# Non-local blocks: layers alternate between images, and the next block's keys and values are made inside the current one

## The chip, the cores and the metric

The kernel runs on one core of one Trainium2 chip. The metric is the device time of one execution in microseconds. Times of several runs are given as their median; one more execution was recorded by the hardware profiler, and all durations below come from that one.

## What is computed

Four images of 128 channels and 96x96 positions pass through two layers of the same form. Cut to one layer, with float32 throughout:

```python
g_x = maxpool2(conv1x1(x, g_w, g_b)).reshape(b, CI, -1).transpose(0, 2, 1)
theta_x = conv1x1(x, theta_w, theta_b).reshape(b, CI, -1).transpose(0, 2, 1)
phi_x = maxpool2(conv1x1(x, phi_w, phi_b)).reshape(b, CI, -1)
f = jnp.einsum('bqc,bck->bqk', theta_x, phi_x)
attn = jax.nn.softmax(f, axis=-1)
y = jnp.einsum('bqk,bkc->bqc', attn, g_x)
y = y.transpose(0, 2, 1).reshape(b, CI, H, W)
W_y = conv1x1(y, W_w, W_b)
inv = bn_gamma * jax.lax.rsqrt(bn_var + BN_EPS)
W_y = W_y * inv[None, :, None, None] + (bn_beta - bn_mean * inv)[None, :, None, None]
return W_y + x
```

CI is 64. An image has 9216 queries and, after the pooling, 2304 keys. Layer 1 reads what layer 0 wrote, so one image's two layers are strictly one after the other; different images do not depend on each other.

## The kernel before

One layer of one image is a *block*; there are eight, in the order image 0 layer 0, image 0 layer 1, image 1 layer 0 and so on (L322 to L326). An image is one SBUF tile x of 128 partitions x 9216, loaded in six pieces (L84); layer 0 writes its result back into it, layer 1 into a tile `out` that is stored (L286).

A block first makes its keys and values (`keys_and_values`, L146). In 24 chunks of 384 positions, `pooled` projects x to g and phi with one matmul of 128x128 weights (L157) into a PSUM buffer of the pool `ps_sc`, and VectorE takes the 2x2 maximum out of PSUM into `gphi` (L160). Three times, after 8 chunks each, `spread` brings phi onto both halves of the partitions on ScalarE (L174, L177, after a centre on VectorE, L170) and transposes g with six TensorE transposes (L180), which VectorE adds the bias to (L183).

Then the block goes over 9 *pairs* of 512 queries (NP, p). `theta` (L198) projects a pair's queries: two matmuls of 128x64 weights, one for each 512 queries, side by side in the array's columns. For each of 18 key tiles (k), `scores` (L219) issues four matmuls in 64x64 quarters of the array, ScalarE takes the exponential of the 128x1024 result (L228), VectorE adds it to a running sum (L232, L234), and `values` (L236) multiplies it by g, again in four 64x64 quarters, into the accumulator `av`. The loop in `block` (L297) goes in steps t of two key tiles: the scores of step t, then the values of step t-1. So TensorE alternates between 16 recorded passes of scores and 16 of values. (A float32 matmul is recorded as two passes.)

Behind a pair come its ending steps. ScalarE copies the accumulator out (`halves`, L249). `denominators` (L251), hung one step behind the pair's last values, sums the sums over partitions with a matrix of ones (`den`, two 128x64 matmuls, L254); VectorE takes four reciprocals from PSUM (L260), adds the halves (L262), multiplies (L263) and keeps a running largest and smallest reciprocal (L264, L265), from which a flag is made at the end that chooses a general routine if the sums went out of range. `project` (L267), three steps later, multiplies by W in two 64x128 matmuls (L275), and VectorE adds shift and x (L281). `theta` of the next pair is called in the middle of a pair. A scheduler of the language places the instructions of each engine by its own estimates; the order in the program is its input. The endings of a block's last pair fall into the next block's key making.

PSUM: `ps_sc` has two buffers of two banks, `ps_av` one of two, and `ps_misc` two of one bank, which `theta`, `den`, `W_ps` and `gT_ps` take in turn.

Of the kernel before, what the change touches and what calls it, by code (L numbers as in the profile page):

```python
# [16 lines left out]
P = 128  # L17
# [18 lines left out]
NB = NKT // KB  # L36
SHIFT = 35.0
# [4 lines left out]
def shifted_blocks(ctx: ExitStack, tc: tile.TileContext, x: bass.AP, layers, out: bass.AP, flag):  # L42
# [11 lines left out]

    nc = tc.nc
# [3 lines left out]
    xp = ctx.enter_context(tc.tile_pool(name="xp", bufs=2))  # L59
# [14 lines left out]
    rmax = const.tile([P, QT], F32, name="rmax")  # L74
    nc.gpsimd.memset(rmax, 1.0)
    rmin = const.tile([P, QT], F32, name="rmin")
    nc.gpsimd.memset(rmin, 1.0)
# [68 lines left out]
    def keys_and_values(xt, w, name):  # L146

        gphi = kvp.tile([P, NK], F32, tag="gphi", name=f"gphi_{name}", bufs=1)  # L150
        phi = kvp.tile([P, NK], F32, tag="phi", name=f"phi_{name}")
        gT = kvp.tile([P, NKT, CI], F32, tag="gT", name=f"gT_{name}")
        centre = kvp.tile([P, 1], F32, tag="centre", name=f"centre_{name}")

        def pooled(r):
            ps = ps_sc.tile([P, PT], F32, tag="sc", name=f"gphi_ps_{name}_{r}")
            nc.tensor.matmul(  # L157
                ps[:, :CC], lhsT=w["gphi"], rhs=xt[:, ts(r, CC)], start=True, stop=True
            )
            nc.vector.tensor_reduce(  # L160
                gphi[:, ts(r, CC // 4)].rearrange("p (h w) -> p h w", w=W // 2),
                ps[:, :CC].rearrange("p (h a w b) -> p h w a b", a=2, b=2, w=W // 2),
                AX.XY,
                ALU.max,
            )

        def spread(i):
# [10 lines left out]
            ps = ps_misc.tile([P, QT], F32, tag="misc", name=f"gT_ps_{name}_{i}")  # L178
            for j in range(GT):
# [4 lines left out]
                gT[:, ts(i, GT), :],  # L184
                ps[:, : GT * CI].rearrange("p (t c) -> p t c", c=CI),
                w["g_b"].rearrange("p (o c) -> p o c", o=1).to_broadcast((P, GT, CI)),
# [3 lines left out]
        per = GT * KT * 4 // CC  # L190
        for r in range(HW // CC):
            pooled(r)
            if r % per == 0 and r:
                spread(r // per - 1)
        spread(NKT // GT - 1)
        return phi, gT

    def theta(xt, w, p, name):  # L198
        ps = ps_misc.tile([P, QT], F32, tag="misc", name=f"theta_ps_{name}_{p}")
        for h in range(2):  # L200
            nc.tensor.matmul(  # L201
                ps[ts(h, CI), :], lhsT=w["theta"], rhs=xt[:, ts(2 * p + h, QT)],
# [439 lines left out]
```

## Time and profile before

| | |
|---|---|
| median of 3 runs | 2765.25 us (2764.35 to 2766.28) |
| the profiled execution, own time | 2764.58 us |
| its span in the profile | 2762.3 us |
| TensorE matmul (PE) busy | 2689.1 us, 97% |
| VectorE (DVE) busy | 2115.4 us, 77% |
| ScalarE (ACT) busy | 1536.5 us, 56% |
| DMA | 41.41 MB, mean 15 GB/s |

The span is the time from the profile's first instruction to its last; 2.3 us of the execution lie outside it. In the views, PE is TensorE's matmuls and PEld its weight loads, which have a row of their own; L12 is a line of the kernel, `av<-exp,gT` says which tile an instruction writes and which it reads. A row of the timeline has a start, the busy time of a group of equal instructions, the engine, line, operation, tiles, and the size of one; "x16" is how many, and in brackets stands how long the engine had been idle and who ended that. A matmul's recorded end is modelled and reaches into its successor, so the cost of a group of matmuls is read from its start to the start of the next. "64*64" is the part of the array that a matmul uses.

### The profile page before, as it was taken

The numbers are of one execution on the slowest core, as the hardware profiler recorded it, in microseconds if no ns is written. First come the engines' busy times: TensorE is split into PE (matmuls) and PEld (weight loads), VectorE is DVE, ScalarE is ACT, GpSimd is POOL, SyncE is SP. The second block draws the span as 40 slices with busy tenths as digits, with TensorE's granted clock in tenths as the row PEclk, the third lists the DMA queues.
The fourth block names the chain that finished last, engine by engine and source line by source line (L and its number), as shares of the span: only waits on it lengthen the run. The fifth ranks groups of instructions, "written<-read, shape, count | busy, mean of one in ns | idle before, by whom it ended". The sixth has DMA issues, their size and how long they took to land.

```text
span 2762.3 us, 50645 instructions
## 1 busy us (share of the span) xinstructions
PE 2689.1 (97%) x22136; PEld 911.1 (33%) x22136; DVE 2115.4 (77%) x2203; ACT 1536.5 (56%) x1492; POOL 1.6 (0%) x8
## 2 busy tenths in 40 slices
PE   7999999999999999999999999999999999999998
PEld 2333333333333333333333333333333333333332
DVE  4777767778677786777867778677786877867777
ACT  3555546555455564555546665455554666456664
POOL 0000000000000000000000000000000000000000
PEclk9999999999999999999999999999999999999999
DMA  4000000000100000000010000000000000000000
GB/s 142 1 1 1 1 1 16 16 17 17 77 1 1 1 1 1 16 17 16 16 77 1 1 1 1 1 17 16 16 17 9 1 1 1 1 1 17 16 16 25
DMA packets 11686, 41.41 MB, mean 15 GB/s; under 512 B 3392, under 2 KB 3776, under 8 KB 11456
## 3 DMA queue, kind: packets, MB, share of 16 engines
q1 hardware_dynamic: 8640, 37.75, 3.5%
q8 instruction: 175, 2.87, 0.4%
q10 hardware_dynamic: 2816, 0.34, 0.1%
q14 instruction: 55, 0.45, 0.1%
HBM read 19.21 MB, written 18.87 MB: 14 GB/s over the span
## 4 chain that ended last, share of the span: by engine, by line
PE 95%; DVE 2%; ACT 1%; DMA 1%; issue 0%; ACTq 0%
PE av L242 41%; PE sc L223 41%; PE gphi_ps L157 5%; PE W_ps L275 3%; PE theta_ps L201 3%; PE den L254 3%; DVE rc L260 1%; PE gT_ps L180 1%; DVE gphi L160 0%; ACT exp L228 0%; DMA W_nat<-in_L_conv_W_w_dram 0%; DVE centre L170 0%; ACT phi L174 0%; ACT phi L177 0%; DMA theta_b<-in_L_conv_theta_b_dram 0%; DMA theta_nat<-in_L_conv_theta_w_dram 0%
## 5 line engine op out<-in xcount | busy, mean ns | idle before, releaser
L228 ACT ACTIVATE exp<-sc,nshift 128x1024 f32<-128x1024 f32 x1296 | 1375.3, 1113 | 835.9 <-PE sc L223 835.7
L234 DVE TENSOR_TENSOR sum<-sum,exp 128x1024 f32<-128x1024 f32 x1152 | 1405.2, 1220 | 365.9 <-ACT exp L228 304.4
L223 PE MATMUL sc<-theta,phi 64*64 64x512 f32 x10368 | 1237.4, 592 | 13.0 <-ACT exp L228 8.4
L242 PE MATMUL av<-exp,gT 64*64 64x512 f32 x10368 | 1230.7, 590 | 0.0
L223 PEld LDWEIGHTS sc<-theta,phi 64*64 64x64 f32 x10368 | 381.6, 133 | 763.2 <-issue 735.7
L242 PEld LDWEIGHTS av<-exp,gT 64*64 64x64 f32 x10368 | 390.0, 133 | 729.2 <-issue 710.2
L260 DVE RECIPROCAL rc<-den 128x128 f32<-128x128 f32 x288 | 243.7, 908 | 12.6 <-PE den L254 12.6
L232 DVE TENSOR_TENSOR sum<-exp,exp 128x1024 f32<-128x1024 f32 x72 | 88.2, 1225 | 153.3 <-ACT exp L228 153.3
L157 PE MATMUL gphi_ps<-x,gphiT 128*128 128x384 f32 x384 | 172.0, 564 | 10.3 <-DVE gphi L160 5.2
L160 DVE TENSOR_REDUCE gphi<-gphi_ps 128x96 f32<-128x384 f32 x192 | 105.4, 556 | 62.3 <-PE gphi_ps L157 56.6
L206 ACT ACTIVATE theta<-theta_ps,theta_b 128x512 f32<-128x512 f32 x72 | 49.5, 688 | 148.5 <-PE theta_ps L201 148.5
L275 PE MATMUL W_ps<-y,WT 64*128 64x512 f32 x288 | 88.9, 696 | 31.5 <-DVE y L263 31.5
L174 ACT ACTIVATE phi<-gphi,centre 64x768 f32<-64x768 f32 x24 | 22.3, 930 | 153.8 <-DVE centre L171 119.4
L249 ACT COPY halves<-av 128x1024 f32<-128x1024 f32 x72 | 72.9, 1012 | 46.4 <-PE av L242 46.4
L157 PEld LDWEIGHTS gphi_ps<-x,gphiT 128*128 128x128 f32 x384 | 69.0, 208 | 78.5 <-DVE gphi L160 46.1
L201 PE MATMUL theta_ps<-x,thetaT 128*64 128x512 f32 x288 | 87.3, 618 | 0.0
L254 PE MATMUL den<-sum,ones 128*64 128x512 f32 x288 | 77.7, 618 | 0.0
L262 DVE TENSOR_TENSOR y<-halves 128x512 f32<-128x512 f32 x72 | 49.3, 685 | 15.5 <-ACT halves L249 15.5
L281 DVE SCALAR_TENSOR_TENSOR x<-W_ps,shift,x 128x512 f32<-128x512 f32 x72 | 53.3, 744 | 2.5 <-PE W_ps L275 2.5
L281 DVE SCALAR_TENSOR_TENSOR out<-W_ps,shift,x 128x512 f32<-128x512 f32 x72 | 53.3, 744 | 2.1 <-PE W_ps L275 2.1
L275 PEld LDWEIGHTS W_ps<-y,WT 64*128 64x128 f32 x288 | 23.3, 198 | 88.6 <-issue 51.2
L265 DVE TENSOR_TENSOR rmin<-rmin,rc 128x512 f32<-128x512 f32 x72 | 49.2, 684 | 0.0
(47 smaller groups left out, 230.1 us busy)
## 6 DMA issues: line engine op xcount, KB each, us to landing
x<-in_x_dram SPq DMA_DIRECT2D x24, 768.0 KB, 8.0
out_dram<-out SPq DMA_DIRECT2D x36, 512.0 KB, 2.6
theta_nat<-in_L_conv_theta_w_dram ACTq DMA_DIRECT2D x2, 32.0 KB, 5.5
theta_b<-in_L_conv_theta_b_dram ACTq DMA_DIRECT2D x4, 0.2 KB, 6.1
gphi_nat<-in_L_conv_g_w_dram ACTq DMA_DIRECT2D x2, 32.0 KB, 5.6
gphi_nat<-in_L_conv_phi_w_dram ACTq DMA_DIRECT2D x2, 32.0 KB, 5.2
g_b<-in_L_conv_g_b_dram ACTq DMA_DIRECT2D x2, 32.0 KB, 5.6
W_nat<-in_L_conv_W_w_dram ACTq DMA_DIRECT2D x2, 32.0 KB, 6.4
```

What stands on the lines that cost most here:

```text
L157: nc.tensor.matmul(ps[:, :CC], lhsT=w["gphi"], rhs=xt[:, ts(r, CC)], start=True, stop=True)
L160: nc.vector.tensor_reduce(gphi[:, ts(r, CC // 4)].rearrange("p (h w) -> p h w", w=W // 2), ps[:, :CC].rearrange("p (h a w b) -> p h w a b" ...
L201: nc.tensor.matmul(ps[ts(h, CI), :], lhsT=w["theta"], rhs=xt[:, ts(2 * p + h, QT)], start=True, stop=True,)
L223: nc.tensor.matmul(ps[ts(c, CI), ts(h, QT)], lhsT=self.phi[ts(h, CI), ts(2 * k + c, CI)], rhs=self.th[ts(h, CI), :], start=True, stop=True,)
L228: nc.scalar.activation(e, ps, AF.Exp, bias=nshift)
L232: nc.vector.tensor_add(self.sum, self.es[0], e)
L234: nc.vector.tensor_add(self.sum, self.sum, e)
L242: nc.tensor.matmul(self.av[ts(h, CI), ts(r, QT)], lhsT=self.gT[ts(r, CI), k, :], rhs=e[ts(r, CI), ts(h, QT)], start=(k == 0), stop=(k == N ...
L254: nc.tensor.matmul(ps[ts(h, CI), :], lhsT=ones, rhs=self.sum[:, ts(h, QT)], start=True, stop=True,)
L260: nc.vector.reciprocal(rc[:, ts(i, P)], ps[:, ts(i, P)])
L275: nc.tensor.matmul(ps, lhsT=self.w["W"][ts(h, CI), :], rhs=self.y[ts(h, CI), :], start=True, stop=True,)
L281: nc.vector.scalar_tensor_tensor(dst[:, ts(h, QT)], pss[h], self.w["shift"], self.xt[:, ts(2 * self.p + h, QT)], op0=ALU.add, op1=ALU.add,)
```

## The change

The diff does the following.

- The blocks come in the order of `ORDER`, so that a block of another image stands between the two layers of an image. Three x tiles are kept instead of two, and both layers write into x in place; the stores read x.
- The eight blocks become one loop over 72 pairs (of 9 steps each). Block n+1's keys and values are made while block n's pairs run: each pair has one *window*, behind the first values of that pair (`J_WINDOW`), in which its predecessor's `den`, three chunks of the next block's `pooled`, and the next pair's `theta` are issued together. A block's three `spread` steps are issued in the windows of its predecessor's pairs 3, 6 and 8; pair 8 has no chunks. The first block's keys are made ahead of the loop, and the last block has no next one to make.
- `pooled` uses two matmuls of 128x64 weights (the g and the phi half) in place of one of 128x128, and its PSUM comes from `ps_misc`, like all that a window writes.
- `den` is copied out of PSUM by ScalarE (`rc`); the reciprocals then read SBUF, and the extremes are two reductions into a column for each pair. All of it stands as one run on VectorE (`normalise`), behind the window's reductions.
- `project` uses four matmuls in 64x64 quarters and comes four steps after the window.
- `exp` has 9 buffers instead of 6; `halves` and `rc` have one instead of two.
- In the loop, TensorE, VectorE and ScalarE keep the order in which the program calls them (`manual_schedule`); the key making ahead of it is still placed by the scheduler. There, TensorE now has the weight transposes of both layers (L102, six of them) ahead of the first chunk; before, ten chunks stood ahead of the last of these (L97, `WT_ps` of layer 1).

The core of the diff:

```diff
+J_WINDOW, J_PROJECT = 0, 4
+CHUNKS = 3
+ORDER = ((0, 0), (1, 0), (0, 1), (2, 0), (1, 1), (3, 0), (2, 1), (3, 1))
...
-    xp = ctx.enter_context(tc.tile_pool(name="xp", bufs=2))
+    xp = ctx.enter_context(tc.tile_pool(name="xp", bufs=3))
...
-            ps = ps_sc.tile([P, PT], F32, tag="sc", name=f"gphi_ps_{name}_{r}")
-            nc.tensor.matmul(
-                ps[:, :CC], lhsT=w["gphi"], rhs=xt[:, ts(r, CC)], start=True, stop=True
-            )
+            ps = ps_misc.tile([P, QT], F32, tag="misc", name=f"gphi_ps_{self.name}_{r}")
+            for h in range(2):
+                nc.tensor.matmul(
+                    ps[ts(h, CI), :CC], lhsT=self.w["gphi"][:, ts(h, CI)],
+                    rhs=self.xt[:, ts(r, CC)], start=True, stop=True,
+                )
...
+        def key_steps(self):
+
+            steps = {}
+            for r in range(HW // CC):
+                steps.setdefault(r // CHUNKS, []).append(lambda r=r: self.pooled(r))
+            for i in range(NKT // GT):
+                last = ((i + 1) * GT * KT * 4 // CC - 1) // CHUNKS
+                steps.setdefault(last + 1, []).append(lambda i=i: self.spread(i))
+            return steps
...
-            rc = work.tile([P, QT], F32, tag="rc", name=f"rc_{self.name}")
+            self.rc = work.tile([P, QT], F32, tag="rc", name=f"rc_{self.name}", bufs=1)
+            nc.scalar.copy(self.rc, ps)
+
+        def normalise(self):
+            rc, n = self.rc, self.number
+            self.y = y = self.halves[:, :QT]
+            nc.vector.tensor_add(y, y, self.halves[:, QT:])
             for i in range(QT // P):
-                nc.vector.reciprocal(rc[:, ts(i, P)], ps[:, ts(i, P)])
...
-            nc.vector.tensor_tensor(rmax, rmax, rc, ALU.max)
-            nc.vector.tensor_tensor(rmin, rmin, rc, ALU.min)
+                nc.vector.reciprocal(rc[:, ts(i, P)], rc[:, ts(i, P)])
+            nc.vector.tensor_mul(y, y, rc)
+            nc.vector.tensor_reduce(rmax[:, n : n + 1], rc, AX.X, ALU.max)
+            nc.vector.tensor_reduce(rmin[:, n : n + 1], rc, AX.X, ALU.min)
...
-                ps = ps_misc.tile([P, QT], F32, tag="misc", name=f"W_ps_{self.name}_{h}")
-                nc.tensor.matmul(
-                    ps, lhsT=self.w["W"][ts(h, CI), :], rhs=self.y[ts(h, CI), :],
-                    start=True, stop=True,
-                )
-                pss.append(ps)
-            for h in range(2):
+                pss.append(ps_misc.tile([P, QT], F32, tag="misc", name=f"W_ps_{self.name}_{h}"))
+            for c in range(2):
+                for h in range(2):
+                    nc.tensor.matmul(
+                        pss[h][ts(c, CI), :], lhsT=self.blk.w["W"][ts(h, CI), ts(c, CI)],
+                        rhs=self.y[ts(h, CI), :], start=True, stop=True,
+                    )
...
+    with tc.manual_schedule(engines=engines):
+        for t in range(total + NB):
+            if t < total:
+                q, j = divmod(t, NB)
+                if q % NP == 0 and j == 0 and q // NP + 1 < len(blocks):
+                    begin(q // NP + 1)
+                    steps = blocks[q // NP + 1].key_steps()
                 for k in range(j * KB, (j + 1) * KB):
...
+                    pairs[q].scores(k)
+            if t == 0:
+                continue
+            q, j = divmod(t - 1, NB)
+            if j == J_PROJECT and q:
+                pairs[q - 1].project()
+            if t <= total:
                 for k in range(j * KB, (j + 1) * KB):
...
+                    pairs[q].values(k)
+            if j == J_WINDOW:
+                others = list(steps.pop(q % NP, [])) if q < len(pairs) else []
+                if q:
+                    pairs[q - 1].denominators()
+                for step in others[:1]:
+                    step()
+                if q + 1 < len(pairs):
+                    pairs[q + 1].theta()
+                for step in others[1:]:
+                    step()
+                if q:
+                    pairs[q - 1].normalise()
```

What that makes of the engines' orders, at three places. First TensorE inside the first block, where pair 2 has just begun. Before, the end of pair 1 (`den_0_0_1`: image 0, layer 0, pair 1; the last number is the buffer's) stands by itself between values (`av`) and scores (`sc`):

```order
L242 MATMUL av_0_0_2_814<-exp_0_0_2_0_777,gT_0_0_204 64x512 x4
L242 MATMUL av_0_0_2_814<-exp_0_0_2_1_784,gT_0_0_204 64x512 x4
L254 MATMUL den_0_0_1_823<-sum_0_0_1_543,ones_92 64x512 x2
L223 MATMUL sc_0_0_2_4_836<-theta_0_0_2_698,phi_0_0_203 64x512 x4
L223 MATMUL sc_0_0_2_5_844<-theta_0_0_2_698,phi_0_0_203 64x512 x4
```

Now, at the same place:

```order
L258 MATMUL av_0_0_2_868<-exp_0_0_2_0_831,gT_0_0_195 64x512 x4
L258 MATMUL av_0_0_2_868<-exp_0_0_2_1_838,gT_0_0_195 64x512 x4
L270 MATMUL den_ps_0_0_1_877<-sum_0_0_1_583,ones_92 64x512 x2
L168 MATMUL gphi_ps_1_0_6_882<-x_1_332,gphiT_0_117 64x384 x2
L227 MATMUL theta_ps_0_0_3_886<-x_0_96,thetaT_0_107 64x512 x2
L168 MATMUL gphi_ps_1_0_7_891<-x_1_332,gphiT_0_117 64x384 x2
L168 MATMUL gphi_ps_1_0_8_895<-x_1_332,gphiT_0_117 64x384 x2
L238 MATMUL sc_0_0_2_4_907<-theta_0_0_2_632,phi_0_0_194 64x512 x4
L238 MATMUL sc_0_0_2_5_915<-theta_0_0_2_632,phi_0_0_194 64x512 x4
```

Three chunks of image 1's keys (`gphi_ps_1_0_6` to `_8`) and the theta of pair 3, which stood nineteen rows behind `den`, have come into one run with `den`.

Second, TensorE where the first block ends. Before, from the last values of pair 8 on:

```order
L242 MATMUL av_0_0_8_2272<-exp_0_0_8_16_2449,gT_0_0_204 64x512 x4
L242 MATMUL av_0_0_8_2272<-exp_0_0_8_17_2457,gT_0_0_204 64x512 x4
L254 MATMUL den_0_0_8_2478<-sum_0_0_8_2244,ones_92 64x512 x2
L157 MATMUL gphi_ps_0_1_0_2501<-x_0_98,gphiT_1_164 128x384
L157 MATMUL gphi_ps_0_1_1_2504<-x_0_98,gphiT_1_164 128x384
L275 MATMUL W_ps_0_0_8_0_2491<-y_0_0_8_2486,WT_0_147 128x512
L275 MATMUL W_ps_0_0_8_1_2493<-y_0_0_8_2486,WT_0_147 128x512
L157 MATMUL gphi_ps_0_1_2_2507<-x_0_98,gphiT_1_164 128x384
L157 MATMUL gphi_ps_0_1_3_2510<-x_0_98,gphiT_1_164 128x384
L180 MATMUL gT_ps_0_1_0_2532<-ident_83,gphi_0_1_2497 128x64
L157 MATMUL gphi_ps_0_1_4_2513<-x_0_98,gphiT_1_164 128x384
L157 MATMUL gphi_ps_0_1_5_2516<-x_0_98,gphiT_1_164 128x384
```

Now, from the first scores of image 1's pair 0 on; `gphi_ps_0_1_0` is the first chunk for image 0's layer 1:

```order
L238 MATMUL sc_1_0_0_0_2649<-theta_1_0_0_2459,phi_1_0_340 64x512 x4
L238 MATMUL sc_1_0_0_1_2656<-theta_1_0_0_2459,phi_1_0_340 64x512 x4
L258 MATMUL av_0_0_8_2432<-exp_0_0_8_16_2626,gT_0_0_195 64x512 x4
L258 MATMUL av_0_0_8_2432<-exp_0_0_8_17_2634,gT_0_0_195 64x512 x4
L238 MATMUL sc_1_0_0_2_2675<-theta_1_0_0_2459,phi_1_0_340 64x512 x4
L238 MATMUL sc_1_0_0_3_2683<-theta_1_0_0_2459,phi_1_0_340 64x512 x4
L258 MATMUL av_1_0_0_2691<-exp_1_0_0_0_2654,gT_1_0_341 64x512 x4
L258 MATMUL av_1_0_0_2691<-exp_1_0_0_1_2661,gT_1_0_341 64x512 x4
L270 MATMUL den_ps_0_0_8_2700<-sum_0_0_8_2404,ones_92 64x512 x2
L168 MATMUL gphi_ps_0_1_0_2705<-x_0_96,gphiT_1_162 64x384 x2
L227 MATMUL theta_ps_1_0_1_2709<-x_1_332,thetaT_0_107 64x512 x2
L168 MATMUL gphi_ps_0_1_1_2714<-x_0_96,gphiT_1_162 64x384 x2
```

The key making that stood between two blocks is gone from there: the next block's scores stand ahead of the last values of the block before, as at any other pair.

Third, VectorE around the end of pair 1, before (`rc` are reciprocals, `sum` the running sums):

```order
L232 TENSOR_TENSOR sum_0_0_2_786<-exp_0_0_2_0_777,exp_0_0_2_1_784 128x1024
L262 TENSOR_TENSOR y_0_0_1_831<-halves_0_0_1_796 128x512
L234 TENSOR_TENSOR sum_0_0_2_786<-sum_0_0_2_786,exp_0_0_2_2_803 128x1024
L234 TENSOR_TENSOR sum_0_0_2_786<-sum_0_0_2_786,exp_0_0_2_3_811 128x1024
L260 RECIPROCAL rc_0_0_1_826<-den_0_0_1_823 128x128 x4
L234 TENSOR_TENSOR sum_0_0_2_786<-sum_0_0_2_786,exp_0_0_2_4_841 128x1024
L263 TENSOR_TENSOR y_0_0_1_831<-y_0_0_1_831,rc_0_0_1_826 128x512
L264 TENSOR_TENSOR rmax_94<-rmax_94,rc_0_0_1_826 128x512
L265 TENSOR_TENSOR rmin_96<-rmin_96,rc_0_0_1_826 128x512
L234 TENSOR_TENSOR sum_0_0_2_786<-sum_0_0_2_786,exp_0_0_2_5_849 128x1024
```

And now:

```order
L250 TENSOR_TENSOR sum_0_0_2_840<-sum_0_0_2_840,exp_0_0_2_2_857 128x1024
L250 TENSOR_TENSOR sum_0_0_2_840<-sum_0_0_2_840,exp_0_0_2_3_865 128x1024
L172 TENSOR_REDUCE gphi_1_0_339<-gphi_ps_1_0_6_882 128x96
L172 TENSOR_REDUCE gphi_1_0_339<-gphi_ps_1_0_7_891 128x96
L172 TENSOR_REDUCE gphi_1_0_339<-gphi_ps_1_0_8_895 128x96
L280 TENSOR_TENSOR halves_0_0_1_850<-halves_0_0_1_850 128x512
L282 RECIPROCAL rc_0_0_1_880<-rc_0_0_1_880 128x128 x4
L283 TENSOR_TENSOR halves_0_0_1_850<-halves_0_0_1_850,rc_0_0_1_880 128x512
L284 TENSOR_REDUCE rmax_94<-rc_0_0_1_880 128x1
L285 TENSOR_REDUCE rmin_95<-rc_0_0_1_880 128x1
L250 TENSOR_TENSOR sum_0_0_2_840<-sum_0_0_2_840,exp_0_0_2_4_912 128x1024
```

The three reductions that free the chunks' PSUM stand behind the sums of key tiles 2 and 3, and the whole normalising run stands behind them and ahead of the sum of key tile 4; before, that sum stood in the midst of it.

More of the change, by code (lines that the diff above doesn't have):

```diff
@@ L73, in shifted_blocks @@
     nc.vector.memset(ones, 1.0)
[L74 to L77, printed above, removed]
+    rmax = const.tile([P, len(ORDER) * NP], F32, name="rmax")
+    rmin = const.tile([P, len(ORDER) * NP], F32, name="rmin")
     def load_x(b):
@@ L165, in pooled, with spread @@
             )
-        def spread(i):
+        def spread(self, i):
+            gphi, phi, centre = self.gphi, self.phi, self.centre
             keys = ts(i, GT * KT)
```

143 lines of the change are left out of this document (60 added, 83 removed).

## Prediction

> **What bounds the kernel now.** I read the page's busy shares and chain first:
>
> ```profile
> span 2762.3 us, 50645 instructions
> PE 2689.1 (97%) x22136; PEld 911.1 (33%) x22136; DVE 2115.4 (77%) x2203; ACT 1536.5 (56%) x1492; POOL 1.6 (0%) x8
> PE 95%; DVE 2%; ACT 1%; DMA 1%; issue 0%; ACTq 0%
> PE av L242 41%; PE sc L223 41%; PE gphi_ps L157 5%; PE W_ps L275 3%; PE theta_ps L201 3%; PE den L254 3%; DVE rc L260 1%; PE gT_ps L180 1%; DVE gphi L160 0%; ACT exp L228 0%; DMA W_nat<-in_L_conv_W_w_dram 0%; DVE centre L170 0%; ACT phi L174 0%; ACT phi L177 0%; DMA theta_b<-in_L_conv_theta_b_dram 0%; DMA theta_nat<-in_L_conv_theta_w_dram 0%
> ```
>
> TensorE ends the run: 82% of the chain is scores and values, which the change keeps. Only the rest can move, so next comes TensorE's timeline through one pair:
>
> ```profile
> 599.77 1.04 PE L242 MATMUL av<-exp,gT 64*64 64x512 f32 x8
> 600.74 1.08 PE L254 MATMUL den<-sum,ones 128*64 128x512 f32 x4
> ...
> 603.51 1.90 PE L242 MATMUL av<-exp,gT 64*64 64x512 f32 x16
> ...
> 608.66 1.90 PE L223 MATMUL sc<-theta,phi 64*64 64x512 f32 x16
> 610.49 1.13 PE L275 MATMUL W_ps<-y,WT 64*128 64x512 f32 x4
> ...
> 613.32 1.90 PE L223 MATMUL sc<-theta,phi 64*64 64x512 f32 x16
> 615.03 1.90 PE L242 MATMUL av<-exp,gT 64*64 64x512 f32 x16
> 616.86 1.08 PE L201 MATMUL theta_ps<-x,thetaT 128*64 128x512 f32 x4
> 617.87 1.95 PE L223 MATMUL sc<-theta,phi 64*64 64x512 f32 x16
> 619.64 1.90 PE L242 MATMUL av<-exp,gT 64*64 64x512 f32 x16
> ```
>
> From 603.51 to 608.66 stand three groups of 16: 1.717 us each, so 0.43 for one pass of 512 columns (four quarters abreast), 0.86 for a key tile. An ending step costs more than its two passes: den (4 records) 603.51 - 599.77 less 0.86 and 1.717, 1.16; theta 4.61 (615.03 to 619.64) less 3.43, 1.18; W 4.66 less 3.43, 1.23. So leaving the 64x64 form and coming back costs 0.31 (0.37 around W). Then the seam between two blocks, on the same timeline:
>
> ```profile
> 352.77 3.61 PE L242 MATMUL av<-exp,gT 64*64 64x512 f32 x32
> ...
> 362.63 2.08 PE L275 MATMUL W_ps<-y,WT 64*128 64x512 f32 x4 [3.75 <-DVE y L263]
> ...
> 389.67 1.95 PE L223 MATMUL sc<-theta,phi 64*64 64x512 f32 x16 [0.57 <-ACT theta L206]
> 392.62 2.09 PE L223 MATMUL sc<-theta,phi 64*64 64x512 f32 x16 [1.01 <-ACT exp L228]
> 394.54 1.04 PE L242 MATMUL av<-exp,gT 64*64 64x512 f32 x8
> ```
>
> The old block's values end at 352.77 + 3.43 = 356.20; the new one's begin at 394.54. Two score groups (3.43) are due there anyway, so a seam costs 34.9, with TensorE idle for y, and then slow: around it the granted clock was half.
>
> ```profile
> 363.00:367.00 4.00, 4.00 (x8) 1.31 (x6) 3.08 (x6) 0.00 (x0) 0.00 (x0) 0.50 0.00 0
> ```
>
> Last the head and the tail:
>
> ```profile
> 28.81 0.25 DVE L142 TENSOR_SCALAR W_bn<-W_nat,inv 128x64 f32<-128x64 f32 x1 [0.38 <-DMA W_nat<-in_L_conv_W_w_dram]
> 29.22 0.27 PE L97 MATMUL WT_ps<-ident,W_bn 128*64 128x128 f32 x1
> 29.42 0.58 PE L180 MATMUL gT_ps<-ident,gphi 64*128 64x64 f32 x6
> 46.91 1.95 PE L223 MATMUL sc<-theta,phi 64*64 64x512 f32 x16 [0.58 <-ACT theta L206]
> ```
> ```profile
> 2742.39 3.61 PE L242 MATMUL av<-exp,gT 64*64 64x512 f32 x32
> 2752.25 2.08 PE L275 MATMUL W_ps<-y,WT 64*128 64x512 f32 x4 [5.24 <-DVE y L263]
> ```
>
> The old run by these terms: 1296 groups x 1.717 = 2225.2; 64 pairs with all three endings x 3.57 = 228.5; 7 seams x 34.9 = 244.3; head 46.9; the first block's fill 1.4 (as at a seam: 394.54 - 389.67 - 3.43); tail 2762.3 - 2745.8 = 16.5. Sum 2762.8 for a span of 2762.3.
>
> **The change, part by part.** *Core*: unchanged, 2225.2.
>
> *W in quarters*: the form of its neighbours, so two passes and no return: 0.86 x 71 = 61.1 (the last pair's lies in the tail). Bounds: 0.86 and today's 1.23; the score groups are the same instruction shape, so 0.86.
>
> *The window*: den, chunk a, theta, chunks b and c. All that is released in it comes from these rows (ScalarE, then VectorE, then a stretch of key making):
>
> ```profile
> 598.35 2.13 ACT L228 ACTIVATE exp<-sc,nshift 128x1024 f32<-128x1024 f32 x2
> 617.99 0.69 ACT L206 ACTIVATE theta<-theta_ps,theta_b 128x512 f32<-128x512 f32 x1 [1.44 <-PE theta_ps L201]
> ```
> ```profile
> 599.50 2.56 DVE L234 TENSOR_TENSOR sum<-sum,exp 128x1024 f32<-128x1024 f32 x2 [0.33 <-ACT exp L228]
> 601.97 3.38 DVE L260 RECIPROCAL rc<-den 128x128 f32<-128x128 f32 x4
> ...
> 606.35 0.68 DVE L263 TENSOR_TENSOR y<-y,rc 128x512 f32<-128x512 f32 x1
> ...
> 608.15 5.21 DVE L234 TENSOR_TENSOR sum<-sum,exp 128x1024 f32<-128x1024 f32 x4
> 613.28 0.74 DVE L281 SCALAR_TENSOR_TENSOR out<-W_ps,shift,x 128x512 f32<-128x512 f32 x1
> ```
> ```profile
> 380.71 3.12 PE L157 MATMUL gphi_ps<-x,gphiT 128*128 128x384 f32 x8
> 381.65 1.20 DVE L160 TENSOR_REDUCE gphi<-gphi_ps 128x96 f32<-128x384 f32 x2
> ```
>
> A chunk is two passes of 384 columns, 2 x 0.43 x 3/4 = 0.64. Unhindered, the window is 0.31 + 2 x 0.86 + 3 x 0.64 = 3.95. But two PSUM buffers serve five tiles, so theta waits for ScalarE's copy of den, b for a's reduction, c for ScalarE's theta. Count from S, the end of the last values (600.63 here, 0.11 ahead of den). Den starts at S+0.11; ScalarE takes such a result 1.13 after its start (616.86 to 617.99) and needs 0.69: den's buffer is free at S+1.98 with 0.05 for the signal. ScalarE is free then: its exponentials end at 600.48. TensorE is through with den at S+1.02 and with a at S+1.66, so theta waits 0.32. Theta runs to S+2.89; b needs a's reduction: a's start S+1.02, plus 0.94 (380.71 to 381.65), plus 0.56, S+2.52, so it is hidden, with 0.37 to spare, if VectorE is free by S+1.96; its sums end at 602.06, S+1.43. b runs to S+3.53. Theta's buffer comes free at S+1.98+1.13+0.69+0.05 = S+3.85: c waits 0.32, ends at S+4.54, and the way back adds 0.15: 4.69. 56 windows x 4.69 = 262.6. Of the 16 without chunks, 15 cost 0.31 + 1.72 = 2.03 and the last, without theta, 1.17: 31.6. The new copy `rc` has no row; its bounds are 0.60 (a 128x512 VectorE operation above) and 1.0; theta's 0.69 is the same engine, size and source.
>
> *Spreads*: six transposes were 0.58 together. In pairs 3 and 6 they stand at the window's end, one more change of form (0.1): 0.7 each; in pair 8, ahead of theta, two more changes, about 0.9. The first of a block also holds ScalarE, which waits for the centre behind c's reduction, past the next exponentials: about 0.7, since the scores after next need their buffers. 3.0 x 7, say 20 in all; without cover by the two score buffers each spread's ScalarE work of some 1.8 would show, 25 more.
>
> *Seams*: gone; the fill of 1.4 stays once. *Mid-pair dens and thetas*: in the window.
>
> *Head*: layer 1's last weight was transposed at 29.22, and ten chunks stood ahead of it; now all 24 stand behind it. Its data landed at 28.8 at the latest, which does not change: the third image is queued behind the first two. 24 chunks at 0.77 (two buffers: 0.69 + 0.23 + 0.56 + 0.06 for two chunks in turn, near the 0.78 of 380.71) are 18.5, two spreads inside some 2.5, last reduction, phi, its copy and theta some 3.8, half a clock for its first microseconds 2: 29.2 + 26.8 = 56, for 46.9. Bounds 47 (as now) and 61.
>
> *Tail*: the reciprocals wait for the copy behind `halves`, but the multiplication comes earlier; 16.
>
> *VectorE*, which hides b and the sums: per pair 17 sums x 1.28 (608.15 to 613.28 for four) = 21.8, normalising 3.38 + 4 x 0.60 = 5.8, two residual adds 1.5, reductions 1.7, and 2.2 idle in the window between S+1.43 and c's reduction: 33.0, of a new period of 18 x 1.717 + 0.86 + 4.69 = 36.5. So it falls behind after a window and has caught up before the next, with 3.5 to spare. Behind the normalising run wait the sums of key tiles 4 on; their exponentials fill buffers that are needed nine tiles later, over 15 us, so ScalarE does not stop.
>
> *Transfers*: two rows of the page, the second with size and time to landing of one piece:
>
> ```profile
> q1 hardware_dynamic: 8640, 37.75, 3.5%
> x<-in_x_dram SPq DMA_DIRECT2D x24, 768.0 KB, 8.0
> ```
>
> On SyncE the last image's load now stands behind the nine stores of the first one, of which the last is issued at the fourth block's start; its first chunk is read at the fifth's, some 330 us later, against six pieces of 8.0. Nothing; without that lead, one load of up to 48.
>
> Sum: 2225.2 + 61.1 + 262.6 + 31.6 + 20 + 56 + 1.4 + 16 = 2673.9 for the span. 2.3 lie outside it, and the median stands 0.7 above the profiled execution: **2677**. What goes is 228.5 + 244.3 + 46.9 + 16.5; what comes is 447.3.
>
> A weight load's cover decides the window too. In the row below den's four loads lie within 0.20, while its second pass starts about 0.48 after the first (1.01 less 0.43 and the 0.10 of the way back): the second pass's loads ran beside the first pass, in the same rows of the array.
>
> ```profile
> 356.32 0.20 PEld L254 LDWEIGHTS den<-sum,ones 128*64 128x64 f32 x4 [0.81 <-DVE sum L234]
> ```
>
> The Trainium skill ("TensorE: Matmul & The Clock Gate", Part 3, what overlaps and what doesn't) says that a weight load runs beside a matmul under way only in another row group, which side-by-side column halves do not have; this row speaks against it.
>
> **The rivals.**
> - *Loads uncovered.* Each pass in the 128x64 form shows its loads, 0.10 by the row above: ten passes, less three already charged at 0.05, 0.85 x 56, and 0.3 x 16: 2729. The Trainium skill's rule just named is this case. Chance 0.03.
> - *No waits in the window*: both 0.32 and their restarts vanish if the releases come earlier than the rows say: 56 x 0.74 = 41 less, 2636. Against it: the order of buffers is fixed. Chance 0.10.
> - *VectorE late in the window.* If its sums end later than S+1.8, b waits, and the delay passes on: 1 us late is 0.63 x 56 = 35 more, 2712; 1.35 late, 2732. For it: the spare of 3.5 is less in the windows with a spread (0.6 to 1.7 more). Chance 0.13.
> - *VectorE becomes the bound; slower.* From 36.5 us a pair on VectorE sets the period: then it never catches up, and chunk b waits for the whole normalising run's remainder. To lose what is won it would need 2770.8 - 2677 over 56 pairs, 1.7 a pair beyond its spare of 3.5: 5.2 more than the 33.0 counted. No row shows that; the reciprocals from SBUF are new, but are 3.4 now. Chance 0.06, a third of it within 0.2% of today.
>
> **How the numbers follow.** 2677 has 0.68, with its own bounds 2655 to 2700 (head down by 9, spreads by 13; spreads up by 20). The range 2636 to 2732 takes in that, the late VectorE and half of the case without waits; left out are 0.05 there, 0.06 and parts of the rest, in all under 0.2. 0.2% of 2765 is 5.5 us, about what a measurement tells from nothing. Faster by more: 0.68 + 0.03 + 0.10 + 0.13 = 0.94; same 0.02; slower 0.04.
>
> **What would show it.** TensorE's timeline: scores, values and W_ps with no gap, a window of about 4.7 from values to scores, theta and c each 0.3 late, PEclk flat after the head, first scores at 56. Wrong: a pair's period well over 36.5, VectorE without idle time, `sc` waiting for `exp`, or chunks waiting for VectorE longer than for ScalarE.

## The result, and the profile after

| | before | after |
|---|---|---|
| median (range) of 4 runs each | 2764.80 us (2763.51 to 2766.28) | 2668.30 us (2665.29 to 2668.97) |
| ratio of the times, 95% interval | | 0.9649 [0.9632, 0.9665] |
| the profiled execution, its span | 2764.58, 2762.3 | 2668.49, 2666.4 |
| mean granted clock | 0.989 | 0.998 |

The kernel became 96.5 us faster: 2668 against a forecast of 2677 and a range of 2636 to 2732. The page of after, its span, busy time and chain:

```profile
span 2666.4 us, 51928 instructions
PE 2607.6 (98%) x22808; PEld 896.0 (34%) x22808; DVE 2131.1 (80%) x2203; ACT 1576.9 (59%) x1564; POOL 0.7 (0%) x6
PE 95%; ACT 3%; DMA 1%; DVE 1%; issue 0%; ACTq 0%
```

TensorE still ends the run. Its busy time fell by 81.5 where the span fell by 95.9: most of the gain is in what the profile counts as TensorE's work, half-clock passes among it, and the smaller part in gaps. (Ends of matmuls are modelled, so short waits inside a window count as busy too.) ScalarE has come onto the chain with 3%, which the windows explain. TensorE's timeline through one window and the W that follows:

```profile
642.15 1.90 PE L258 MATMUL av<-exp,gT 64*64 64x512 f32 x16
643.98 1.08 PE L270 MATMUL den_ps<-sum,ones 128*64 128x512 f32 x4
644.89 0.81 PE L168 MATMUL gphi_ps<-x,gphiT 128*64 128x384 f32 x4
645.74 1.08 PE L227 MATMUL theta_ps<-x,thetaT 128*64 128x512 f32 x4
646.65 1.82 PE L168 MATMUL gphi_ps<-x,gphiT 128*64 128x384 f32 x8
648.40 1.95 PE L238 MATMUL sc<-theta,phi 64*64 64x512 f32 x16
...
660.47 1.04 PE L294 MATMUL W_ps<-halves,WT 64*64 64x512 f32 x8
661.33 1.90 PE L258 MATMUL av<-exp,gT 64*64 64x512 f32 x16
...
680.32 1.08 PE L270 MATMUL den_ps<-sum,ones 128*64 128x512 f32 x4
```

W costs 661.33 - 660.47 = 0.86, with no gap: two passes. The window goes from the values' end, S = 642.15 + 1.717 = 643.87, to 648.40 and 0.05 for a first pass of scores that is that much longer: 4.58. Den starts at S + 0.11 and takes two passes of 0.43 and the 0.05 of a first one (0.91, to 644.89). Chunk a's own two passes are 0.64, and theta starts 0.85 after it: 0.21 late. Theta is 0.91, b and c together 1.75, where two unhindered chunks are 1.28 and the way back some 0.15: 0.32 late. From one den to the next lie 36.34; over the whole trace this period is 36.35 in every pair with a plain window. The two releases, on ScalarE:

```profile
645.10 0.59 ACT L275 COPY rc<-den_ps 128x512 f32<-128x512 f32 x1 [1.39 <-PE den_ps L270]
646.87 0.69 ACT L232 ACTIVATE theta<-theta_ps,theta_b 128x512 f32<-128x512 f32 x1 [1.18 <-PE theta_ps L227]
```

Den's buffer is free at 645.10 + 0.59, 645.69, and theta's first matmul starts at 645.74. Theta's is free at 647.56, and c starts just behind. The view of waits has both (us in total, times, longest), about once for each window with chunks:

```profile
PEld gphi_ps L168 <- ACT theta L232: 45.2, 56, 0.8
PEld theta_ps L227 <- ACT rc L275: 41.1, 62, 0.7
```

VectorE in the same pair:

```profile
649.00 0.68 DVE L280 TENSOR_TENSOR halves<-halves 128x512 f32<-128x512 f32 x1
649.60 3.38 DVE L282 RECIPROCAL rc<-rc 128x128 f32<-128x128 f32 x4
...
666.57 5.20 DVE L250 TENSOR_TENSOR sum<-sum,exp 128x1024 f32<-128x1024 f32 x4
672.17 2.55 DVE L250 TENSOR_TENSOR sum<-sum,exp 128x1024 f32<-128x1024 f32 x2 [0.39 <-ACT exp L244]
676.61 1.23 DVE L248 TENSOR_TENSOR sum<-exp,exp 128x1024 f32<-128x1024 f32 x1 [1.89 <-ACT exp L244]
679.09 1.22 DVE L250 TENSOR_TENSOR sum<-sum,exp 128x1024 f32<-128x1024 f32 x1 [1.26 <-ACT exp L244]
```

From the normalising run at 649.00 it works without a break and has caught up at 671.77. The idle times behind that, 0.39 + 1.89 + 1.26 = 3.54, are its spare before the next window. Where before had a seam, the stretch around the first change of block now looks like any other (busy time of PE, PEld, DVE, ACT, POOL, then the granted clock):

```profile
377.00:395.00 18.00, 17.82 (x152) 5.83 (x148) 11.56 (x14) 10.48 (x11) 0.00 (x0) 1.00 0.00 1
```

Head and tail, last:

```profile
29.20 0.26 DVE L147 TENSOR_SCALAR W_bn<-W_nat,inv 128x64 f32<-128x64 f32 x1 [1.11 <-DMA W_nat<-in_L_conv_W_w_dram]
```
```profile
29.86 9.80 PE L168 MATMUL gphi_ps<-x,gphiT 128*64 128x384 f32 x40
...
55.76 1.95 PE L238 MATMUL sc<-theta,phi 64*64 64x512 f32 x16 [1.26 <-ACT theta L232]
...
2647.21 3.61 PE L258 MATMUL av<-exp,gT 64*64 64x512 f32 x32
...
2656.80 1.98 PE L294 MATMUL W_ps<-halves,WT 64*64 64x512 f32 x8 [4.96 <-DVE halves L283]
```

The first chunk waits for layer 1's last weight, as forecast; first scores stand at 55.76, and the last values end at 2650.64, 15.8 ahead of the end.

### The profile page after: what moved, and what is told of

Read it like the earlier page. It is cut to its first block, busy times and chain, and to the rows that moved or that the text cites. A ratio compares the mean times of both kernels' runs of the same rounds, so it can differ in the third digit from the quotient of the medians.

```text
span 2666.4 us, 51928 instructions
## 1 busy us (share of the span) xinstructions
PE 2607.6 (98%) x22808; PEld 896.0 (34%) x22808; DVE 2131.1 (80%) x2203; ACT 1576.9 (59%) x1564; POOL 0.7 (0%) x6
## 4 chain that ended last, share of the span: by engine, by line
PE 95%; ACT 3%; DMA 1%; DVE 1%; issue 0%; ACTq 0%
PE sc L238 42%; PE av L258 41%; PE gphi_ps L168 4%; PE theta_ps L227 3%; PE den_ps L270 3%; PE W_ps L294 2%; ACT theta L232 1%; DMA W_nat<-in_L_conv_W_w_dram 0%; ACT exp L244 0%; DVE centre L186 0%; ACT phi L190 0%; DVE gphi L172 0%; ACT phi L193 0%; DMA theta_b<-in_L_conv_theta_b_dram 0%; DMA theta_nat<-in_L_conv_theta_w_dram 0%
## 5 line engine op out<-in xcount | busy, mean ns | idle before, releaser
L282 DVE RECIPROCAL rc<-rc 128x128 f32<-128x128 f32 x288 | 243.4, 907 | 0.0
L168 PE MATMUL gphi_ps<-x,gphiT 128*64 128x384 f32 x768 | 160.5, 502 | 8.9 <-DVE gphi L172 0.7
L300 DVE SCALAR_TENSOR_TENSOR x<-W_ps,shift,x 128x512 f32<-128x512 f32 x144 | 101.0, 743 | 0.5 <-PE W_ps L294 0.5
L168 PEld LDWEIGHTS gphi_ps<-x,gphiT 128*64 128x64 f32 x768 | 48.7, 137 | 124.1 <-ACT theta L232 45.2
L294 PE MATMUL W_ps<-halves,WT 64*64 64x512 f32 x576 | 75.7, 596 | 5.0 <-DVE halves L283 5.0
L270 PE MATMUL den_ps<-sum,ones 128*64 128x512 f32 x288 | 77.7, 618 | 0.0
L283 DVE TENSOR_TENSOR halves<-halves,rc 128x512 f32<-128x512 f32 x72 | 49.8, 692 | 2.5
L280 DVE TENSOR_TENSOR halves<-halves 128x512 f32<-128x512 f32 x72 | 49.1, 682 | 1.6 <-ACT halves L265 1.6
L284 DVE TENSOR_REDUCE rmax<-rc 128x1 f32<-128x512 f32 x72 | 48.9, 678 | 0.0
L285 DVE TENSOR_REDUCE rmin<-rc 128x1 f32<-128x512 f32 x72 | 48.6, 676 | 0.0
```

The costliest lines, as they stand in the source:

```text
L168: nc.tensor.matmul(ps[ts(h, CI), :CC], lhsT=self.w["gphi"][:, ts(h, CI)], rhs=self.xt[:, ts(r, CC)], start=True, stop=True,)
L270: nc.tensor.matmul(ps[ts(h, CI), :], lhsT=ones, rhs=self.sum[:, ts(h, QT)], start=True, stop=True,)
L282: nc.vector.reciprocal(rc[:, ts(i, P)], rc[:, ts(i, P)])
L294: nc.tensor.matmul(pss[h][ts(c, CI), :], lhsT=self.blk.w["W"][ts(h, CI), ts(c, CI)], rhs=self.y[ts(h, CI), :], start=True, stop=True,)
L300: nc.vector.scalar_tensor_tensor(dst, pss[h], self.blk.w["shift"], dst, op0=ALU.add, op1=ALU.add)
```

## Experiments

Each was timed in several rounds beside the kernel before, whose median was 2762.4 to 2763.6 in these rounds. A ratio carries about 0.0016 either way, so two kernels of different rounds compare to some 4 to 5 us; where a smaller difference matters, the period of a pair (start of den to start of the next den) is read from the traces; for one kind of window it repeats to about 0.01 us within a trace, except where VectorE sets it (the run with eight extra operations).

| kernel | median (range), us | ratio to before, 95% |
|---|---|---|
| after | 2668.30 (2665.29 to 2668.97) | 0.9649 [0.9632, 0.9665] |
| W in halves | 2691.77 (2689.45 to 2694.37) | 0.9743 [0.9727, 0.9759] |
| before, order alone | 2762.94 (2759.74 to 2765.60) | 1.0001 [0.9992, 1.0011] |
| before, order and late endings | 2723.10 (2721.93 to 2724.29) | 0.9858 [0.9842, 0.9875] |
| keys at once | 2655.49 (2654.60 to 2656.52) | 0.9613 [0.9597, 0.9629] |
| two more buffers | 2632.71 (2631.52 to 2633.74) | 0.9529 [0.9513, 0.9545] |
| theta apart | 2667.41 (2666.32 to 2669.84) | 0.9657 [0.9641, 0.9673] |
| layer 1 loaded late | 2661.66 (2660.45 to 2663.46) | 0.9639 [0.9623, 0.9655] |
| 3 more on VectorE | 2671.15 (2669.97 to 2671.96) | 0.9671 [0.9655, 0.9688] |
| 8 more on VectorE | 2761.50 (2758.77 to 2763.51) | 0.9991 [0.9981, 1.0000] |
| more buffers, layer 1 late | 2627.97 (2625.90 to 2628.13) | 0.9508 [0.9491, 0.9525] |

### What the W tiles are worth

After, with W as it was, two 64x128 matmuls:

```diff
-            for c in range(2):
-                for h in range(2):
-                    nc.tensor.matmul(
-                        pss[h][ts(c, CI), :], lhsT=self.blk.w["W"][ts(h, CI), ts(c, CI)],
...
+            for h in range(2):
+                nc.tensor.matmul(
+                    pss[h], lhsT=self.blk.w["W"][ts(h, CI), :],
...
```

> The changed kernel with one part undone: W is again two 64x128 matmuls among the 64x64 scores and values. Theory (each leaving of the 64x64 form costs TensorE about 0.37 us around W, with nothing else to hide it): 71 times 0.37 is 26, so 2668 becomes about 2694, with 1.23 from the scores before W to the values behind it, less their own time. Rival (the form of W matters little, the gain is all at the seams): 2668 to 2673.

Measured 2691.77: 23.5 more. The period went from 36.35 to 36.71, and 71 x 0.36 = 25.6. W takes as many passes in either kernel, and after has one change of form less: the theory holds. The 64x128 form also has longer weight loads, 0.19 for 0.13 us, and this run does not part the two; den and theta, with loads of 0.13, cost 0.31 by themselves, so most of the 0.36 goes with the form.

### What the seams are worth, and what the new order alone does

First, before with nothing but the new order of blocks, three x tiles, and the stores reading x:

```diff
...
-    for b in range(B):
-        nxt = load_x(b + 1) if b + 1 < B else None
-        block(xt, ws[0], None, f"{b}_0")
-        block(xt, ws[1], out[b].rearrange("c h w -> c (h w)"), f"{b}_1")
-        xt = nxt
+    for n, (b, l) in enumerate(order):
+        nb = order[n + 1][0] if n + 1 < len(order) else b
+        if nb not in xs:
+            xs[nb] = load_x(nb)
+        store = out[b].rearrange("c h w -> c (h w)") if l else None
+        block(xs[b], ws[l], store, f"{b}_{l}")
...
```

> The kernel before with the blocks in the new order, three x tiles and stores out of x, and nothing else. Theory (alternating the images by itself moves no instruction: TensorE and VectorE have the same order at the seam with another image's name): 2765, within 5. Rival (the seam waits for the last pair's output, which the next layer of the same image reads): 7 times the 3.8 of idle time and what the half clock costs, 2720 to 2740.

Measured 1.0001 [0.9992, 1.0011], clock 0.989 as before. Alternating the images buys nothing by itself; VectorE's order still has the old pair's normalising run ahead of the new block's reductions. Its first seam, on TensorE and VectorE:

```profile
356.36 1.56 PE L157 MATMUL gphi_ps<-x,gphiT 128*128 128x384 f32 x4
361.67 2.08 PE L272 MATMUL W_ps<-y,WT 64*128 64x512 f32 x4 [3.75 <-DVE y L263]
```
```profile
356.48 3.39 DVE L260 RECIPROCAL rc<-den 128x128 f32<-128x128 f32 x4 [1.58 <-PE den L254]
...
362.13 1.02 DVE L160 TENSOR_REDUCE gphi<-gphi_ps 128x96 f32<-128x384 f32 x2
```

Two chunks fill the two buffers by 358; VectorE reduces them at 362.13, behind the whole normalising run, and TensorE stands for 3.75 in between. The row puts TensorE's wait down to y, because W stands ahead of the third chunk in its order; but without W the third chunk would have waited for its buffer until about 362.7 (362.13 and one reduction of 0.56). Both waits are for the same run. Then the same with the last pair's den, normalising and W hung behind the next block's first values instead (the keys and values still made in one go between the blocks):

```diff
...
-        for key in sorted(hooks):
-            for step in hooks[key]:
-                step()
+        den, project = [step for key in sorted(hooks) for step in hooks[key]]
+        return {(1, "columns"): [den], (4, "rows"): [project]}
...
```

> The kernel before, with the blocks in the new order, three x tiles and stores out of x, and the endings of a block's last pair (den, normalising, W) carried behind the next block's first values; the key making stays at the seam, all matmuls keep their old forms. Theory (TensorE's idle time at the seam is VectorE's normalising run standing ahead of the chunks' reductions, and the half clock follows from it): a seam falls from 34.9 to about 26.2 with 2.4 of endings moved into a pair, 7 times 6.3 is 44, 2721 (2710 to 2735), and the granted clock no longer drops at the seams. Rival (the seam is bound by key latency, not by the endings): within 10 of 2765.

Measured 2723.10, 39.8 below the run with the order alone, in the theory's range. TensorE's first seam, and the stretch around it with the granted clock:

```profile
351.75 3.61 PE L242 MATMUL av<-exp,gT 64*64 64x512 f32 x32
355.29 2.48 PE L157 MATMUL gphi_ps<-x,gphiT 128*128 128x384 f32 x6
357.92 1.56 PE L157 MATMUL gphi_ps<-x,gphiT 128*128 128x384 f32 x4 [0.15 <-DVE gphi L160]
...
385.16 1.90 PE L242 MATMUL av<-exp,gT 64*64 64x512 f32 x16
386.99 1.08 PE L254 MATMUL den<-sum,ones 128*64 128x512 f32 x4
```
```profile
355.00:381.00 26.00, 24.87 (x82) 10.44 (x82) 16.33 (x30) 5.95 (x7) 0.00 (x0) 1.00 0.00 1
```

The seam is 385.16 - 355.18 - 3.43 = 26.6 for 34.9. The den and the W that now stand among the pairs cost 2.4 of the 8.3 again, so 5.9 a seam are won, 7 x 5.9 = 41. The gap is 0.15 instead of 3.75, and the clock stays at 1.00. So the stop and the half-clock spell behind it are one cost, and both come from the place of the old pair's endings, not from the place of the chunks. The run moves den, the normalising run and W together and does not weigh them one by one. The period across this seam is 59.83, for 34.46 elsewhere, so a block's keys, with the refilling of the pipeline, cost 25.4 at a seam that has no stop.

(The Trainium skill, "TensorE: Matmul & The Clock Gate", HAM oscillation, warns of idle gaps over about 3.4. At the seams the trace agrees: behind each gap of 3.75 the clock was 0.50, and behind the gaps of 1.01 of this run it was not. Elsewhere the clock fell behind shorter ones: with layer 1 loaded late, below, it was 0.50 from 25.9 to 32.6, behind a gap of 2.89, and with both together from 47.0 to 53.5, with no gap over 0.6 in the 17 us before. So staying under 3.4 does not by itself keep the clock up here.)

### Whether spreading the keys thinly gains

After, with all 24 chunks and three spreads of the next block in the window of pair 8:

```diff
+            if self.name != "0_0":
+                steps = {NP - 1: [step for n in sorted(steps) for step in steps[n]]}
```

> The changed kernel with all 24 chunks and three spreads of the next block in one window, pair 8's, in place of three chunks in each of eight. Theory (what the change removes is the wait behind the normalising run, the slow clock and the key latency at the seam, and not that chunks lie thinly spread): a run of chunks at 0.76 each is 18.3, the spreads 3, against 8 times 2.56 and 2.8 now, so 2655 to 2670. Rival (spreading the chunks thinly under the pairs is what hides them): a good part of the old seams comes back, 7 times 10 or more, 2740 and up.

Measured 2655.49: 12.8 less than after, and the rival falls. Eight periods of 33.79 and one of 55.58 make 325.9 a block; after has six of 36.35, then 37.90, 36.86 and 34.69, 327.55. Over nine times 33.79, the keys of a block cost 21.8 in one go and 23.4 spread out: the thin windows pay their two waits and the starts around them eight times a block. So how evenly the chunks lie gains nothing. That it matters instead to have scores and values to go on with behind the chunks fits both kernels, but no run tests it by itself.

### Whether the windows wait for PSUM

After, with chunks a and b of each window in buffers of the scores' pool `ps_sc`, so that three tiles share the two small buffers:

```diff
+            if self.spare and r % CHUNKS < 2:
+                ps = ps_sc.tile([P, PT], F32, tag="sc", name=f"gphi_ps_{self.name}_{r}")
+            else:
+                ps = ps_misc.tile([P, QT], F32, tag="misc", name=f"gphi_ps_{self.name}_{r}")
```

> The changed kernel with the first two chunks of each window in the PSUM buffers of the scores, which are idle in the window; theta and the third chunk then find their own buffer free. Theory (the 0.21 and 0.32 that theta and the third chunk still wait, and 0.10 of restarts, are waits for two PSUM buffers): 56 times 0.63 is 35 less, about 2633, the window 3.95 to 4.0 instead of 4.59. Rival (the time between these groups is a cost of the column form or of its weight loads): no change, 2668.

Measured 2632.71, as the theory had it. TensorE in the window:

```profile
633.11 1.90 PE L262 MATMUL av<-exp,gT 64*64 64x512 f32 x16
634.94 1.08 PE L274 MATMUL den_ps<-sum,ones 128*64 128x512 f32 x4
635.85 0.82 PE L172 MATMUL gphi_ps<-x,gphiT 128*64 128x384 f32 x4
636.49 1.03 PE L231 MATMUL theta_ps<-x,thetaT 128*64 128x512 f32 x4
637.35 1.46 PE L172 MATMUL gphi_ps<-x,gphiT 128*64 128x384 f32 x8
638.74 1.95 PE L242 MATMUL sc<-theta,phi 64*64 64x512 f32 x16
```

From S = 634.83 the window is 3.96; chunk a takes 0.64, theta 0.86, b and c 1.39: no wait is left. That is the prediction's unhindered 3.95. The period is 35.72 for 36.35, and 0.63 x 55 = 34.6 of the 35.6. No weight load shows either: ten passes in the 128x64 form cost what their columns cost. The rule that the prediction quoted (the Trainium skill, "TensorE: Matmul & The Clock Gate", Part 3) would add 0.85 to a window, by the prediction's sum; this window, at 3.96, contradicts it.

### Whether theta gains by standing in the window

After, with theta by itself behind the values of step 6:

```diff
-                if q + 1 < len(pairs):
-                    pairs[q + 1].theta()
...
+            if j == 6 and q + 1 < len(pairs):
+                pairs[q + 1].theta()
```

> The changed kernel with theta out of the window, by itself behind the values of step 6, as it stood by itself before. Theory (a separate theta pays 0.31 for the change of form, but without it in the window one of the two buffer waits and a restart go): the window falls from 4.59 to about 3.36 and theta costs 1.18, so 56 times 0.05 less and 15 times 0.31 more: 2668 to 2673, no change that counts. Rival (bringing theta into the window is worth its change of form): 71 times 0.31, 2690.

Measured 2667.41; the period is 36.29 for 36.35. Theta apart pays one more change of form and spares the window its waits, to the same sum. With two buffers, the merged window's gain is given back whole. In the last block, where windows have no chunks, the gain stays: 33.79 a period with theta in the window, 34.10 with theta apart.

### The head

After, with layer 1's weights loaded and prepared behind the first block's keys:

```diff
-    ws = [load_layer(l, p) for l, p in enumerate(layers)]
+    ws = {0: load_layer(0, layers[0])}
...
+    ws[1] = load_layer(1, layers[1])
```

> The changed kernel with layer 1's weights prepared behind the first block's chunks instead of ahead of them. Theory (the first scores come 9 us later than before because 24 chunks wait for layer 1's last weight at 29.5): they come at 44 to 48 again, 2656 to 2661. Rival (the image's own loading sets the head): first scores stay at 55 or so, 2668.

Measured 2661.66; in the traces the first scores come 8.1 earlier and the span is 8.1 shorter, all other periods being equal. TensorE, then VectorE:

```profile
15.70 5.94 PE L168 MATMUL gphi_ps<-x,gphiT 128*64 128x384 f32 x24
24.53 3.07 PE L168 MATMUL gphi_ps<-x,gphiT 128*64 128x384 f32 x12 [2.89 <-DVE gphi L172]
28.81 4.03 PE L168 MATMUL gphi_ps<-x,gphiT 128*64 128x384 f32 x12 [1.21 <-DVE gphi L172]
...
47.68 1.95 PE L238 MATMUL sc<-theta,phi 64*64 64x512 f32 x16 [0.79 <-ACT theta L232]
```
```profile
23.84 0.16 DVE L140 TENSOR_TENSOR shift<-W_b,mean 128x1 f32<-128x1 f32 x1 [3.13 <-DMA mean<-in_L_conv_bn_mean_dram]
...
28.04 0.25 DVE L147 TENSOR_SCALAR W_bn<-W_nat,inv 128x64 f32<-128x64 f32 x1 [1.91 <-DMA W_nat<-in_L_conv_W_w_dram]
28.21 1.01 DVE L172 TENSOR_REDUCE gphi<-gphi_ps 128x96 f32<-128x384 f32 x2
```

The chunks start at 15.70 instead of 29.86, but 14 earlier becomes 8: the scheduler put layer 1's small steps onto VectorE ahead of reductions, where they wait for layer 1's late inputs, 3.13 for the mean and 1.91 for the weight. TensorE's gaps of 2.89 and 1.21 are waits for the reductions behind them, and from 25.9 to 32.6 the granted clock was 0.50. The mechanism holds; the time lies just above the theory's range.

### VectorE's spare

Three, then eight more multiplications of 128x512 in each normalising run, whose result nobody reads:

```diff
+            for i in range(8):
+                nc.vector.tensor_mul(extra, rc, rc)
```

> The changed kernel with three more 128x512 multiplications in each normalising run, whose result nobody reads: 1.8 us of VectorE a pair. Theory (VectorE has about 3.5 us a pair to spare and nothing on TensorE waits for the normalising run): no change, 2665 to 2672. Rival (VectorE already sets part of the period in the window): 72 times up to 1.8, 2700 to 2795.

> The changed kernel with eight more 128x512 multiplications in each normalising run, whose result nobody reads: 4.8 us of VectorE a pair. Theory (from 3.5 us more a pair on VectorE sets the period, through the reductions that free the chunks' buffers): 1.3 beyond the spare in 56 pairs, 73 more, about 2740 (2700 to 2760). Rival (the spare is larger, since VectorE's waits inside the window fill up as well): under 2690.

With three, 2671.15: the first 70 periods are those of after to 0.01 us, what differs lies in the head and behind the last window. With eight, 2761.50: all that was won is gone, ratio 0.9991 [0.9981, 1.0000], more than the theory's 2740 and just above its range. TensorE, VectorE and a row of the waits:

```profile
624.87 1.08 PE L228 MATMUL theta_ps<-x,thetaT 128*64 128x512 f32 x4
627.37 1.51 PE L169 MATMUL gphi_ps<-x,gphiT 128*64 128x384 f32 x8 [1.42 <-DVE gphi L173]
```
```profile
624.29 2.55 DVE L251 TENSOR_TENSOR sum<-sum,exp 128x1024 f32<-128x1024 f32 x2
626.76 0.55 DVE L173 TENSOR_REDUCE gphi<-gphi_ps 128x96 f32<-128x384 f32 x1
...
634.61 5.76 DVE L286 TENSOR_TENSOR extra<-rc 128x512 f32<-128x512 f32 x8
640.29 0.68 DVE L287 TENSOR_REDUCE rmax<-rc 128x1 f32<-128x512 f32 x1
```
```profile
PEld gphi_ps L169 <- DVE gphi L173: 131.8, 76, 2.5
```

The mechanism is the prediction's: the sums run late, chunk a's reduction stands behind them (VectorE has no idle time ahead of it now), and chunk b waits for that. Two sizes were off. Eight extra operations cost 640.29 - 634.61 = 5.68, 0.71 each and not 0.60. And the theory left out the tail: the last values end at 2729.5 of 2761.1, 31.6 ahead of the end for 15.8, since the late sums and the eight operations come behind them. The 70 periods together are 77.9 longer, about 1.1 to 1.3 for a plain pair, so some 4.5 of 5.7 were absorbed: the spare of 3.5 and about 1 of what VectorE idles inside the window.

### More buffers and layer 1 late, together

> The changed kernel with two chunks of each window in the scores' PSUM buffers and with layer 1's weights prepared behind the first block's chunks. Theory (both savings are on TensorE's path and do not overlap): 35 and 9 less, 2622 to 2626. Rival (with the window's waits gone VectorE's reductions come up next and take part of it back): 2630 to 2650.

Measured 2627.97, ratio 0.9508 [0.9491, 0.9525]: 40.3 below after, where the two gains were 35.6 and 6.6. It is the fastest version here, 1.5% below after. By the median it lies 2 us from either theory; the trace decides. A plain window's period is 35.72, as with more buffers alone, so VectorE takes nothing back, and the first scores come at 47.66, as with layer 1 loaded late alone (47.68). The 2 us are lost right behind that, before the first values:

```profile
47.66 6.65 PE L242 MATMUL sc<-theta,phi 64*64 64x512 f32 x32 [0.79 <-ACT theta L236]
```

The first values start at 54.14, 6.48 behind the first scores, and with layer 1 loaded late alone 4.34 behind them; from 47.0 to 53.5 the granted clock was 0.50. So the theory holds in the windows and in the head, and a spell of half clock took the 2 us. Why the clock fell there, no run shows.

## Why the prediction was right, point by point

| term | forecast | measured |
|---|---|---|
| core, 1296 x 1.717 | 2225.2 | 2225.2 |
| W, 71 x 0.86 | 61.1 | 60.9 |
| 56 windows with chunks | 262.6 | 256.9 (4.59 each) |
| 16 windows without | 31.6 | 31.6 |
| spreads, 7 blocks | 20 | 20.7 |
| head and fill | 57.4 | 56.7 |
| tail | 16 | 15.8 |
| sum | 2673.9 | 2667.8 |

The measured sum stands 1.4 above the span of 2666.4; 1.1 of that is the first window, which has no den and takes 3.46. So of the 9 between forecast and median, 6.1 lie in the terms and 1.4 in this excess; most of the rest is that the median stands 1.9 above the span, not the 3.0 that the forecast added. The terms come from the timeline and from the periods: 36.35 = 18 x 1.717 + 0.86 + 4.59 for a plain window, 33.79 for the last block's, so 2.03 without chunks; 1.55, 0.51 and 0.90 more for a block's three spreads.

- *W* held, and the experiment on it gives 0.36 a pair, its old price less its new one.
- *The window* is the one term that was mis-sized: 4.69 forecast, 4.59 measured, 5.7 of the 6.1 by which the sums differ. The step that failed is the copy `rc`, which had no row and was taken at theta's 0.69; it takes 0.59, so theta is 0.21 late and not 0.32. Below the lower bound of 0.60, too: the value lay nearer to the VectorE row than to ScalarE's own. The second wait, 0.32, came as counted.
- *The spreads* came to 20.7 for 20, in part by luck: the second kind cost 0.51 where 0.7 was forecast, the first 1.55 where it was 1.4.
- *The seams* went, all 244 of them, and the forecast did not need to know why a seam cost 34.9. Its wording was narrower than the cause: TensorE was "idle for y", but the run with the order alone shows the chunks' reductions waiting behind the same normalising run, and the one with late endings that moving the old pair's endings is worth 5.9 of the 34.9 a seam, clock included. The other 29 were chunks, spreads, fill, and the last pair's den and W, of which after pays most again in its windows.
- *The head* came as counted, 55.76 for 56. Between traces of kernels with the same head it lies from 53.6 to 57.1, so about 2 of this agreement is luck.
- *Rivals.* No waits: not in this kernel, but it is what two more buffers make, and its price of 41 was 36. VectorE late: the sums were through at S + 1.43 as counted; the spare of 3.5 was 3.54 by the row. Slower through VectorE: eight extra operations, 5.7 us, bring back the time of before, where the rival had put 5.2. Loads uncovered: the window without waits rules it out.

Where the 96.5 went: 24 to 26 are the W tiles (experiment), 40 the stop and the half clock at the seams (experiment). The rest comes out of the periods, and for the most part no experiment weighs it by itself. Den and theta cost 2.03 in a window without chunks and 2.34 apart, 71 x 0.31 = 22 (theta apart costs that 0.31 in the last block). A block's keys cost 23.4 in the windows, the two waits included, and 25.4 at a seam without the stop, 7 x 2.0 = 14. The first block's fill and the tail give about 2.5, and the head takes 8.9 back. With 25.6 and 41 for the two experiments, as the periods have them, that makes 96; the spans differ by 95.9.

## What to carry to other kernels

When a phase between two blocks looks long, see first which engine's program order its first waits follow: here the stop at the seam went when the old pair's endings were issued later, without moving the phase at all. When work of several kinds is merged into one window, count the tiles against the buffers that the window owns, with the reader's time of release for each: five tiles in two buffers gave back 0.63 of every window, and an idle pool next to it held the cure. And price the engine that hides a step by its idle time behind the last burst (3.54 here): three extra operations, some 2.1, left the periods as they were, and eight, 5.7, lost what the change had won.

## What the runs showed of the hardware

- A PSUM copy of 128x512 on ScalarE takes 0.59 us, the activation with a bias of the same size 0.69.
- Eight VectorE multiplications of 128x512 in a row, each reading `rc` twice and writing the same tile, take 5.68 us, 0.71 each; the halves' addition of this size was followed after 0.60 (649.00 to 649.60).
- In the window with two more buffers, 128x64 matmuls side by side in the columns cost their columns and nothing for their weights: 0.64 for two passes of 384, 0.86 for two of 512, where a weight load takes 0.14.
- The granted clock fell to 0.50 behind TensorE's idle gaps of 3.75 at seven seams, but in the head also behind 2.89, and once with no gap over 0.6 in the 17 us before.
